# A convolution phase's written plan: statistics wanted a tile ahead, new durations, and two rows moved into the last product of an MLP

## The chip, the cores and the metric

The kernel runs on one core of one Trainium2 chip. The metric is the device time of one execution in microseconds: 9876.48 us is the median of three runs of the kernel before (9865.71 to 9877.53). The profiled execution spans 9870.0 us.

## What is computed

The input is x of 64 x 96 images of 56 x 56 pixels, in float32. Layer 0 is normalized in groups of three channels, and each of the 6144 images gets its own 7 x 7 filter from a small MLP over its own pixels; the filtered image is added to x. The kernel keeps g alone: adding x is adding the group's deviation to the middle tap and its mean to the bias. Layer 1 (a Fourier mixer and a quantized feed-forward) follows on the result. Only layer 0 is touched here:

```python
g = gn(x)                                       # groups of 3 channels: (x - m) / sqrt(s + eps)
a = g.reshape(b, c, h * w)
a = (a - mu) * rsqrt(var + EPS) * ln_gamma + ln_beta
a = gelu(einsum('bcn,nd->bcd', a, w0) + b0)     # 3136 pixels -> 512
weight = (einsum('bcd,dk->bck', a, w1) + b1).reshape(b * c, 1, 7, 7)
out = conv_general_dilated(g, weight, padding=3, feature_group_count=b * c)
return x + out + attn_bias
```

## The kernel before, in words

`conv_layer` (L299) works on tiles of 126 images, 49 of them (the last has 96), one image per partition. A tile goes through these steps; the names are the functions inside `tile_` (L364):

- **load** brings 126 x 3136 pixels into `x` (two buffers) and a bias column into `sm`, a tile of twelve columns of per-image numbers (four buffers).
- **The statistics** are a chain of small steps over four engines. `stats` x7 and `aggregate` (VectorE) give mean and variance per image; `group_mean` (TensorE, L405) averages over three channels; `spread` (VectorE); `group_variance` (TensorE, L415); `deviation` (ScalarE, a square root, L420); `scales` (VectorE, L425 to L429); `deviation2` (ScalarE, a second root, L432); `inverse2`; `norm` (ScalarE, L438) rewrites the whole of `x`; `rows` (TensorE, L443) turns three columns of `sm` into rows, and `keep_rows` (VectorE) puts them into the tile `rows`. The GELU comes later on ScalarE from another table set, so each tile loads the table for the root and the one for the GELU anew.
- **turn(k)** and **keep_turned(k)**, k from 0 to 6: TensorE transposes four slices of 112 pixels of `x`, ScalarE copies them into `xT` (one buffer).
- **hidden(k)**: the MLP's first product, four of 28 matmuls over 112 pixels each, summed in the bank `pm` (L474). With k = 0 comes one matmul ahead of them (L470): the three rows of `rows` against `rows0`, which brings in mean, bias and scale. `gelu`, `turn_hidden`, `keep_hidden`, `taps`, `keep_taps` make the 49 taps of each image.
- **The convolution by Fourier transforms**: `over_y(k)` (L519) transforms along one axis; `keep_y` and `store_y` write to a scratch tensor in HBM (`turn_x`). For four blocks q: `load_y`, `filter_spectrum` (L537, spectrum of the taps), `over_x` (L565), four products on VectorE (`times`, L572), two sums on GpSimd (`join`, L580), `back_x` (L590), `store_x` to a second scratch tensor (`turn_y`). For seven chunks c: `load_x` into `V` (two buffers), `back_y` (L613), `finish`, `store`.

Banks of PSUM: six under the tag `ps` that turn, over_y, filter, over_x, back_x and back_y share, one for `pm`, one for the small results of the statistics (`pg`).

The order is made in two steps. `Plan` (L167) is a planner in the kernel: `add` takes a step with a due time `when`, an engine, a cost, what it reads and writes, and a `lag` until its result can be used. `emit` keeps a clock of its own and always calls, on each free engine, the ready step with the earliest due time, if its buffers fit and its due time is no more than `ahead` past the earliest step not yet begun. Only the order of the calls comes out of it; nothing waits for a planned time. The recording layer below then makes the semaphores, and places instructions on each engine's queue by its own order of readiness, so that an instruction can stand elsewhere in its queue than its call stood. On the chip each queue is worked through as it stands.

In the plan before, tile i is due from T = 62 i, the statistics are due from T - 25 to T - 10 with costs from 0.15 to 0.85 us (the root with its table load 0.3), and all seven turns from T - 8 to T - 2.

## Time and profile before

| what | value | from |
|---|---|---|
| median of three runs | 9876.48 us | times |
| TensorE busy, whole span | 93% | page, part 1 |
| VectorE, ScalarE, GpSimd busy | 46%, 45%, 17% | page, part 1 |
| 0 to 4300 us: TensorE busy, granted clock | 3849.67 us, 0.85 | table by stage |
| 4300 to 9870 us: TensorE busy, granted clock | 5341.72 us, 0.96 | table by stage |
| matmuls of `hidden` (L474) | 2744 records of 595 ns | page, part 5 |
| mean share of the DMA engines, 0 to 4300 us | 0.42 | table by stage |

A group of instructions reads: line, engine, operation, what it writes and reads, shape, count, then busy time and mean of one, then the idle time of its engine just before it and what ended that. In the list of waits each line is who waited, for whom, the total, the count and the longest. A float32 matmul shows as two records. PE is TensorE, PEld its weight loads, DVE VectorE, ACT ScalarE, POOL GpSimd; SPq is the queue from which the transfers are issued. The granted clock is the share of full speed that TensorE was given. The line numbers of the changed kernel are 4 to 17 higher than before.

### The profile page before, as it was taken

The page shows a single profiled execution, that of the slowest core. Times are in us where ns is not written, and L with a number is a line of the kernel's source. Part 1 is how long each engine was busy: PE and PEld are TensorE (multiplying, and loading weights), DVE is VectorE, ACT ScalarE, POOL GpSimd, SP SyncE. Part 2 cuts the span into 40 slices and gives each one's busy share as a digit, 9 for nine tenths or more (in the row PEclk, how much of TensorE's full clock was granted, in tenths as well). Part 3 has the DMA queues.
Part 4 walks back from the last instruction along what each step waited for, and adds up shares of the span by engine and source line. Part 5 has one row for each costly group of instructions (what it writes and reads, how often), then busy time and mean ns, then how long its engine had stood idle before and what let it go on. Part 6 is the DMA issues. An engine that isn't in the chain of part 4 may idle for free.

```text
span 9870.0 us, 164798 instructions
## 1 busy us (share of the span) xinstructions
PE 9191.4 (93%) x62665; PEld 5769.7 (58%) x62665; DVE 4517.7 (46%) x11547; ACT 4424.6 (45%) x9809; POOL 1691.7 (17%) x1804
## 2 busy tenths in 40 slices
PE   7899999988999889989999999999999999999998
PEld 3545555554554455556666666666666666666665
DVE  2222222222222222225666666666666666666666
ACT  2222222222222222225555555555555555555555
POOL 0111111111111111111222222222222222222222
PEclk9888888888888888869999999999999999999999
DMA  3444444444444444443444444444444444444443
GB/s 105 126 125 122 116 121 121 122 120 126 125 115 119 119 121 122 122 116 107 121 122 120 123 118 124 121 115 119 122 121 123 121 121 121 123 118 118 121 120 94
DMA packets 1164289, 1178.26 MB, mean 119 GB/s; under 512 B 673247, under 2 KB 1075455, under 8 KB 1150932
## 3 DMA queue, kind: packets, MB, share of 16 engines
q1 hardware_dynamic: 1152643, 1160.72, 42.8%
q10 hardware_dynamic: 10858, 7.01, 0.3%
q8 instruction: 498, 8.16, 0.3%
q14 instruction: 290, 2.38, 0.1%
HBM read 589.36 MB, written 578.03 MB: 118 GB/s over the span
## 4 chain that ended last, share of the span: by engine, by line
PE 84%; ACT 5%; DMA 5%; DVE 3%; POOL 1%; issue 1%; ACTq 0%; DVEq 0%; SPq 0%; POOLq 0%
PE pm L474 11%; PE s L1037 8%; PE h L906 6%; PE pf L537 6%; PE s L954 5%; PE s L565 4%; PE s L590 4%; DMA V<-turn_y 4%; PE s L1108 4%; PE c L1197 4%; PE quarters L873 4%; PE s L1113 3%; PE y L1184 3%; PE m L1300 3%; PE m L1322 3%; PE s L1126 3%
## 5 line engine op out<-in xcount | busy, mean ns | idle before, releaser
L474 PE MATMUL pm<-w0g,xT 112*126 112x512 f32 (+1 forms) x2744 | 1242.2, 595 | 46.2 <-ACT xT L463 46.2
L572 DVE TENSOR_TENSOR t<-s,W 128x504 f32<-128x504 f32 (+1 forms) x784 | 490.9, 673 | 1610.1 <-PE s L565 1129.6
L580 POOL TENSOR_TENSOR t<-t,t 128x504 f32<-128x504 f32 (+1 forms) x392 | 485.2, 1245 | 3796.4 <-DVE t L572 3793.3
L474 PEld LDWEIGHTS pm<-w0g,xT 112*126 112x126 f32 (+1 forms) x2744 | 511.2, 188 | 693.4 <-issue 637.4
L1037 PE MATMUL s<-dft,Y 112*128 112x112 f32 (+1 forms) x7552 | 884.1, 299 | 6.1 <-ACT t L963 3.4
L1037 PEld LDWEIGHTS s<-dft,Y 112*128 112x128 f32 (+1 forms) x7552 | 741.2, 182 | 160.3 <-issue 117.9
L1341 POOL TENSOR_TENSOR o<-t,y 96x448 f32<-96x448 f32 x448 | 502.9, 1129 | 1404.7 <-DVE y L1332 1384.1
L906 PE MATMUL h<-w1c,t 96*56 96x193 f32 x3584 | 729.1, 340 | 0.0
L905 PE MATMUL h<-w1c,t 96*64 96x193 f32 x3584 | 722.3, 341 | 0.0
L620 ACT ACTIVATE o<-s,sm 126x448 f32<-126x448 f32 (+1 forms) x343 | 217.6, 634 | 1098.5 <-PE s L613 883.7
L526 DVE COPY A<-s 128x504 f32<-128x504 f32 (+1 forms) x343 | 232.8, 679 | 1041.4 <-PE s L519 1041.4
L1307 ACT CAST h<-m 128x448 f16<-128x448 f32 x1344 | 672.5, 539 | 76.4 <-PE m L1300 62.7
L938 DVE SCALAR_TENSOR_TENSOR g<-h,st,nb 120x192 f32<-120x192 f32 x1792 | 623.4, 410 | 11.5
L893 POOL TENSOR_TENSOR sq<-t 96x448 f32<-96x448 f32 x448 | 466.9, 1047 | 943.4 <-PE quarters L873 685.1
L1310 DVE TENSOR_SCALAR h<-h,fb 128x448 f16<-128x448 f16 x1344 | 458.7, 342 | 369.2 <-ACT h L1307 329.0
L537 PEld LDWEIGHTS pf<-wT,spec 49*128 49x128 f32 x3136 | 543.5, 268 | 128.7 <-issue 111.8
L954 PE MATMUL s<-g,dft 56*64 56x192 f32 x7168 | 583.1, 349 | 21.3 <-DVE t L1191 19.6
L1058 POOL TENSOR_SCALAR w<-w 128x448 f32<-128x448 f32 (+3 forms) x512 | 248.1, 485 | 2026.8 <-DVE w L1052 1743.6
L1052 DVE SCALAR_TENSOR_TENSOR p<-s,pa,p 128x448 f32<-128x448 f32 (+3 forms) x512 | 273.4, 534 | 689.6 <-ACT r L1049 525.9
L537 PE MATMUL pf<-wT,spec 49*128 49x126 f32 (+1 forms) x3136 | 581.0, 362 | 0.4 <-ACT wT L512 0.4
L545 ACT COPY W<-pf 128x504 f32<-128x504 f32 (+1 forms) x392 | 226.2, 577 | 759.8 <-PE pf L537 759.8
L1108 PE MATMUL s<-w2b,CD 128*112 128x192 f32 x1920 | 519.0, 352 | 5.0 <-DVE CD L1052 3.1
(166 smaller groups left out, 17088.0 us busy)
## 6 DMA issues: line engine op xcount, KB each, us to landing
turned<-t SPq DMA_DIRECT2D x896, 180.0 KB
Y<-turned SPq DMA_DIRECT2D x768, 168.0 KB
turn_x<-A SPq DMA_DIRECT2D x336, 252.0 KB
Y<-turn_x SPq DMA_DIRECT2D x768, 110.2 KB
turn_y<-B SPq DMA_DIRECT2D x192, 441.0 KB
V<-turn_y SPq DMA_DIRECT2D x336, 252.0 KB
U<-turned SPq DMA_DIRECT2D x448, 180.0 KB
t<-x SPq DMA_DIRECT2D x448, 168.0 KB
```

Source lines behind the costliest of these rows:

```text
L474: nc.tensor.matmul(v["pm"][:n], v["xT"][:, e * ROWS : e * ROWS + n], w0g[:, e], start=False, stop=e == HALF - 1,)
L537: nc.tensor.matmul(v["pf", q, r][:, f * ROWS : f * ROWS + n], spec[:, q, f, r], v["wT"][:, :n], start=True, stop=True,)
L572: nc.vector.tensor_tensor(blocks(v["t", q, r, s]), blocks(v["s2", q, r][:, : 4 * ROWS]), blocks(v["W", q][:, s]), ALU.mult,)
L580: nc.gpsimd.tensor_tensor(blocks(v["t", q, *a]), blocks(v["t", q, *a]), blocks(v["t", q, *b]), ALU.add if r else ALU.subtract,)
L905: nc.tensor.matmul(out_[:64], rows_[:, :64], moving, start=True, stop=True)
L906: nc.tensor.matmul(out_[64 : 64 + S], rows_[:, S : 2 * S], moving, start=True, stop=True)
L938: nc.vector.scalar_tensor_tensor(v["g"][:, j], v["ps"][:TOK, j, :H1], v["st"][:, 1, j : j + 1], nb1[:TOK], ALU.mult, ALU.max,)
L954: nc.tensor.matmul(v["pd", wp][64 * half : 64 * half + 64, i], dft1[rows_, 4 * c + j], v["g"][rows_, j], start=True, stop=True,)
L1037: nc.tensor.matmul(to_, v["Y"][:, k, channels], dft2, start=True, stop=k0 + k > 0,)
L1108: nc.tensor.matmul(two, cdb, w2b, start=True, stop=False)
L1307: nc.scalar.copy(v["h16", c][:, m], v["u", c, m])
L1341: nc.gpsimd.tensor_tensor(o, t, y, ALU.add)
```

## The change

Three things are done, all in `conv_layer`.

1. **Statistics a tile ahead.** The load is due at T - 85 in place of T - 60, the statistics from T - 72 to T - 40 with gaps between the steps, so that each small step has time to come back before the next engine needs it. `ahead` grows from 110 to 260.
2. **New durations and times.** Costs and lags are set anew (the root with its table load 1.6, TensorE steps with a lag of 0.2). A tile is due every 70 us instead of 62. The turns, the transforms along y and the products of the MLP are spread evenly, one group of each every 8.6 us, and the later steps follow from there. Only the first turn now opens `xT`, so turning no longer waits in the plan for the products before it.
3. **Mean and bias rows in the last product.** L470 goes. The last of the 28 products takes 114 rows instead of 112: `place_rows`, a transfer of two rows of up to 126 numbers on the SP queue, puts two rows of `rows` under the last slice of `xT`, and once, at the start, two rows of `rows0` are put under the last slice of `w0g`. The third row of `rows0` is zero and is left out.

The diff, cut to its core:

```diff
-    plan = Plan(BUFS1, ahead=110.0)
+    plan = Plan(BUFS1, ahead=260.0)
...
-        w0g = cp.tile([RI, HALF, HID0], F32, name="w0g")
+        w0g = cp.tile([RI + 2, HALF, HID0], F32, name="w0g")
...
+        nc.sync.dma_start(w0g[RI:, HALF - 1], rows0[:2])
...
+            def place_rows():
+                nc.sync.dma_start(
+                    v["xT"][RI:, (HALF - 1) * ROWS : (HALF - 1) * ROWS + n], v["rows"][:2, :n]
+                )
...
             def hidden(k):
                 if k == 0:
                     v["pm"] = bank(f"pm{i}", "mlp")
-                    nc.tensor.matmul(
-                        v["pm"][:n], v["rows"][:, :n], rows0, start=True, stop=False
-                    )
                 for e in range(4 * k, 4 * k + 4):
+                    p = RI + 2 if e == HALF - 1 else RI
                     nc.tensor.matmul(
-                        v["pm"][:n], v["xT"][:, e * ROWS : e * ROWS + n], w0g[:, e],
-                        start=False, stop=e == HALF - 1,
+                        v["pm"][:n], v["xT"][:p, e * ROWS : e * ROWS + n], w0g[:p, e],
+                        start=e == 0, stop=e == HALF - 1,
                     )
...
+            def pe(when, cost, step, **kw):
+                add(when, "PE", cost, step, lag=0.2, **kw)
...
-            add(T - 60, "SP", 0.6, load, w=[xs, sm], lag=12.0)
+            add(T - 85, "SP", 0.7, load, w=[xs, sm], lag=8.5)
             for j in range(NCHUNK):
-                add(T - 25 + j, "DVE", 0.62, lambda j=j: stats(j), r=[xs], w=[st])
+                add(T - 72 + j, "DVE", 0.56, lambda j=j: stats(j), r=[xs], w=[st])
...
-            add(T - 17, "PE", 0.2, group_mean, r=[sm], w=[pg])
-            add(T - 16, "DVE", 0.5, spread, r=[pg], w=[sm])
-            add(T - 15, "PE", 0.2, group_variance, r=[sm], w=[pg])
-            add(T - 14, "ACT", 0.3, deviation, r=[pg], w=[sm])
-            add(T - 13, "DVE", 0.85, scales, w=[sm])
-            add(T - 12, "ACT", 0.3, deviation2, w=[sm])
-            add(T - 11.5, "DVE", 0.18, inverse2, w=[sm])
-            add(T - 11.8, "ACT", 2.95, norm, r=[sm], w=[xs])
-            add(T - 11, "PE", 0.15, rows, r=[sm], w=[pg])
+            add(T - 62, "PE", 0.35, group_mean, r=[sm], w=[pg], lag=1.5)
+            add(T - 58, "DVE", 0.7, spread, r=[pg], w=[sm], lag=0.5)
+            add(T - 55, "PE", 0.35, group_variance, r=[sm], w=[pg], lag=1.5)
+            add(T - 51, "ACT", 1.6, deviation, r=[pg], w=[sm], lag=0.3)
+            add(T - 48, "DVE", 0.8, scales, w=[sm], lag=0.3)
+            add(T - 46, "ACT", 0.3, deviation2, w=[sm], lag=0.3)
+            add(T - 44, "DVE", 0.18, inverse2, w=[sm])
+            add(T - 40, "ACT", 3.05, norm, r=[sm], w=[xs], lag=0.3)
+            add(T - 43, "PE", 0.2, rows, r=[sm], w=[pg], lag=1.0)
...
-                add(T - 8 + k, "PE", 0.7, lambda k=k: turn(k), r=[xs], w=[pt, nm("xT")])
-                add(T - 7 + k, "ACT", 0.6, lambda k=k: keep_turned(k), r=[pt],
-                    w=[nm("xT")] + [("xTpart", i, k)])
+                pe(T - 9 + K * k, 0.6, lambda k=k: turn(k), r=[xs],
+                   w=[pt, nm("xT")] if k == 0 else [pt])
+                if k == 0:
+                    add(T - 6, "SP", 0.4, place_rows, r=[nm("rows"), nm("xT")],
+                        w=[("xTrows", i)], lag=2.5)
+                add(T - 8 + K * k, "ACT", 0.58, lambda k=k: keep_turned(k),
+                    r=[pt, nm("xT")], w=[("xTpart", i, k)])
...
-                add(T + 3 * k, "PE", 3.5 + (0.9 if k == 0 else 0),
-                    lambda k=k: hidden(k), r=[nm("xT"), xTk, nm("rows")], w=[nm("mlp")])
+                pe(T + K * k, 3.6, lambda k=k: hidden(k),
+                   r=[nm("xT"), xTk] + ([("xTrows", i)] if k == NCHUNK - 1 else []), w=[nm("mlp")])
...
-                Q = T + 34 + 14 * q
+                Q = M + 12 + 15 * q
...
-                R = T + 108 + 8.5 * c
+                R = M + 12 + 60 + 16 + 8.6 * c
...
-            tile_(i, 62.0 * i)
+            tile_(i, 70.0 * i)
```

Here K is 8.6 and M is T + 6.5 K + 4, the time at which the GELU is due.

## The prediction

> **What bounds the kernel now.** I read the page first (busy shares, clock row), then the table by stage, then the waits of one long stretch, then the timeline of one tile. The page says TensorE:

> ```profile
> span 9870.0 us, 164798 instructions
> PE 9191.4 (93%) x62665; PEld 5769.7 (58%) x62665; DVE 4517.7 (46%) x11547; ACT 4424.6 (45%) x9809; POOL 1691.7 (17%) x1804
> PEclk9888888888888888869999999999999999999999
> ```

> VectorE and ScalarE are below half busy. The convolution takes the first 17 to 18 slices, about 4300 us, and there the granted clock is 8 tenths against 9 later. The change lies in that phase. The second phase's order of TensorE instructions is the same in both built programs, so I leave its 5550 us alone.

> The waits from 500 to 4000 us, which hold 40 tiles (columns: total us, times, longest):

> ```profile
> PE pg L443 <- ACT sm L432: 150.5, 38, 4.0
> ...
> PE s L613 <- DMA V<-turn_y: 72.5, 40, 3.6
> ...
> PE pm L474 <- ACT xT L463: 40.9, 41, 1.0
> ...
> PE pg L415 <- DVE sm L412: 28.0, 40, 0.7
> ```

> Per tile TensorE stands still 3.96 us at L443 (158.4 us of idle time in the group of L443, two waits filed under the DMA included, over 40), 1.81 for the first loads of V, 1.02 for xT, 0.70 at L415, 0.3 elsewhere: 7.8 us. L443 starts 12 times between 1506.3 and 2459.6 us, so a tile takes 86.7 us. How the 3.96 arises, in the timeline:

> ```profile
> 1586.88 1.28 ACT L420 ACT_TABLE_LOAD   x1
> ...
> 1587.67 0.59 PE L415 MATMUL pg<-sm,group 126*126 126x1 f32 x2 [0.70 <-DVE sm L412]
> 1588.29 0.26 ACT L420 ACTIVATE sm<-pg,eps 126x1 f32<-126x1 f32 x1
> ...
> 1588.98 3.00 ACT L438 ACTIVATE x<-x,sm 126x3136 f32<-126x3136 f32 x1 [0.42 <-DVE sm L426]
> ...
> 1592.22 0.37 PE L443 MATMUL pg<-ident,sm 126*3 126x126 f32 x1 [3.96 <-ACT sm L432]
> ...
> 1592.52 3.63 PE L565 MATMUL s<-Y,fwd_x 112*64 112x504 f32 x8
> ```

> L405, L415 and L443 stand back to back on TensorE, and ScalarE runs the 3.00 us normalization ahead of the small root (L432, 0.28 us, ends at 1592.16) that L443 needs. The table load is already over when L415 ends. The last line shows a second cost: eight records of L565 take 3.63 us here, 1.91 at 1525.23. Windows of 4 us (seventh column: clock):

> ```profile
> 1588.00:1592.00 4.00, 0.26 (x2) 0.17 (x1) 0.52 (x4) 3.44 (x4) 0.00 (x0) 0.50 0.79 173
> ...
> 1604.00:1608.00 4.00, 4.00 (x13) 2.03 (x11) 0.00 (x0) 0.58 (x1) 0.00 (x0) 0.50 0.00 0
> ...
> 1612.00:1616.00 4.00, 4.00 (x11) 1.60 (x11) 1.42 (x3) 0.00 (x0) 2.45 (x2) 1.00 0.68 177
> ```

> The clock is whole or half, and stays at half well after the stall.

> [...]half-clock stretches last 7 to 9 times 3.41 us per tile, with a single full window inside some. It starts before the L443 wait, after the last hidden product, in a run of back_y, L470, the V wait and transposes; and filter_spectrum alone (L537) doesn't end it, over_x and back_x do.[...]

> Price of half clock: mean clock in the phase is 0.845, so 2 x 0.155 = 31% of 86.7 = 26.9 us per tile at half. Some 5 of these are waiting; 21.9 are work, which takes 1.85 times as long (3.71/1.95 back_x, 3.78/2.05 filter, 3.63/1.91 over_x), so 21.9 x (1 - 1/1.85) = 10.1 us per tile are lost.

> **The change, part by part.** What counts is the changed program's order on each engine, for nearly every tile (here tile 12 of the steady part; L409, L419, L447 are the old L405, L415, L443):

> ```
> PE   L544 filter q0 (tile 11) | L481 hidden(1) x4 (12) | L409 L419 L447 (13) | L620 back_y 0 (10)
>      | L460 turn 2, L526 over_y 2 (12) | L597 back_x q0 (11) | L620 | L460 | L544 filter q1 | L481 hidden(2)
> ACT  L424 LoadActFuncSet [waits PE] | L424 root | L442 normalize | L436 root | L627 | L467 xT
> ```

> *Due times and durations of the statistics.* They should pull the five small steps apart; the built order does not follow. The three matmuls are still adjacent, and the normalization is still ahead of the second root. Worse, the table load now carries the wait on L419, so its 1.28 us no longer hide: 3.96 + 1.28 = 5.24 us, and 0.70 before. Everything on TensorE queues behind it. Bounds: 3.96 (load hidden after all) to 5.3; I take 5.24.

> *V.* In before the late V loads queue behind the 1543 KB x load (V issued at 1574.60, used at 1581.92). In the new order the V load for block 6 is issued ahead of x, and the first ones about 10 us of TensorE work before use (filter 2.05, hidden 3.6, statistics). The wait goes: -1.81.

> *xT.* over_y 2 directly follows turn 2 and waits for its copy: 1.0 us, as before. Other copies have 1.2 to 6 us of work between. back_x has 5 us or more of TensorE work against about 4.4 for four products (0.68) and a join (1.25): 0.1.

> Idle: 0.70 + 5.24 + 1.02 + 0.1 = 7.1 against 7.8: gain 0.7 us per tile.

> *The removed matmul L470*: 1.12 us in the timeline (1579.71), every tile, on the bounding engine: gain 1.1. Two more rows in the last of 28 products cost nothing: a product's 595 ns come from its 512 columns. The new transfer of two rows has no price of its own in the trace; between a queue slot of 0.3 us and the 7.3 us that the x load needs (1573.73 to 1581.01), it is wanted only by hidden(6), some 60 us of TensorE work after hidden(0), so nothing. The wait of its issue on hidden(6) of the tile before holds the SP queue (behind it: a store of B, loads of Y and V), which have over 10 us.

> *The clock.* The low stretch now starts when hidden(1) ends: 0.58 + 0.70 + 0.58 + 5.24 + 0.37 = 7.5 us[...]. But dense work follows sooner. At half rate: back_y 1.9, turn 1.1, wait 1.0, then over_y 2.2 and back_x 3.7, dense from 11.5 to 17.4. A window of which three quarters were dense released the clock in before, so release falls at 14.2 to 17.7, mean 16. That is 11.4 us at half, 3.5 of them idle; 7.9 x 0.46 = 3.6 us lost. Two new stretches (back_y, turn, filter: 1.03 + 0.6 + 2.05 = 3.7 us)[...]; a quarter each at 2.5 us: 1.3. Lost 4.9 against 10.1: gain 5.2, the largest and least sure term.

> Sum: 0.7 + 1.1 + 5.2 = 7.0 us per tile. The first three tiles have another order; 46 x 7.0 = 322 us. 9876.5 - 322 = 9554, say 9555. Ends of the phase: the last tile's chain is the same steps with a few more back_y in between; nothing.

> **Rivals.**
> 1. [...]2 x 2.5 instead of 1.3, clock gain 1.5. 3.3 x 46 = 152: 9725. For: filter alone closed it. Against: 2.7 us of filter and turn never did.
> 2. [...]gain 0.7 + 1.1 + 10.1 = 11.9, 547 us: 9330. Against: 7.5 us without dense work.
> 3. The statistics wait vanishes as the due times intend: idle 1.1, so 6.7 + 1.1 + 10.1 = 17.9, 823 us: 9053. The order speaks against it.
> 4. Slower: two of the next tile's statistics now stand ahead of the four products of q3 on VectorE and wait for the x load. It needs 7.3 us; the order gives about 10 from turn 6 to the products. If it comes 4 us late, back_x of q3 waits[...]: 7.6 against 7.0, so +28: 9904.

> **How the numbers follow.** Main 0.62, rival 1 0.17, rival 2 0.08, rival 3 0.03, rival 4 0.10 (a part of it within 0.2%, 20 us). Predicted 9555. Range 9400 to 9750: takes in rival 1 and half the way to rival 2, leaves out 0.2. Faster 0.88 (main, 1, 2, 3, less a little), same 0.04, slower 0.08.

> **What would show it.** Right: a wait of about 5.2 us at L447 on the second root, with the table load inside it; no V wait; the xT wait at 1.0; mean clock of the phase near 0.91; tiles of about 79.7 us. Wrong: tiles under 76 us with no wait at L447 (rival 3), clock still near 0.85 (rival 1), or a long wait of back_x on POOL (rival 4).

## The result, and the profile after

The changed kernel takes 9464.63 us (median; 9452.38 to 9472.47) against 9871.09 us for the kernel before, measured beside it: a ratio of 0.9588, 95% interval 0.9571 to 0.9605. The forecast was 9555 us with a range of 9400 to 9750: right in direction and inside the range, 90 us too slow.

The page of the changed kernel first: its span, TensorE's busy time, and the granted clock in 40 slices.

```profile
span 9457.8 us, 164686 instructions
...
PE 8851.2 (94%) x62567; PEld 5498.1 (58%) x62567; DVE 4521.8 (48%) x11547; ACT 4409.0 (47%) x9809; POOL 1687.8 (18%) x1804
...
PEclk9999999999999999799999999999999999999999
```

The convolution phase now ends at 3899 us instead of 4307. TensorE is as full as before, with 340 us less of busy time, although it issues only 49 matmuls less (98 records, two for each): most of what went is the same work, done faster. The clock row says why, since its first part held mostly 8s before.

TensorE's waits between 500 and 3500 us (who waits, for whom, total us, times, longest):

```profile
PE pg L447 <- ACT sm L436: 206.7, 39, 5.3
PE pg L419 <- DVE sm L416: 27.3, 39, 0.7
PE s L526 <- ACT xT L467: 26.1, 39, 0.7
PE s L597 <- POOL t L587: 0.7, 2, 0.4
```

No wait for V is left. The wait on the second root did not go: it grew to 5.3 us in every tile. The timeline of one tile shows it whole (start, duration, engine, line; in brackets the idle time before it and what ended that). L481 is hidden, L419 and L447 are the second and the third small matmul, L424 and L436 the two roots, L442 is the normalization, L526 over_y, L597 back_x:

```profile
1516.60 3.70 PE L481 MATMUL pm<-w0g,xT 112*126 112x512 f32 x8
...
1521.11 0.38 PE L419 MATMUL pg<-sm,group 126*126 126x1 f32 x2 [0.70 <-DVE sm L416]
...
1521.57 1.28 ACT L424 ACT_TABLE_LOAD   x1 [4.29 <-PE pg L419]
...
1523.55 3.00 ACT L442 ACTIVATE x<-x,sm 126x3136 f32<-126x3136 f32 x1 [0.42 <-DVE sm L430]
...
1526.46 0.28 ACT L436 ACTIVATE sm<-sm,eps 126x1 f32<-126x1 f32 x1
...
1526.79 0.37 PE L447 MATMUL pg<-ident,sm 126*3 126x126 f32 x1 [5.30 <-ACT sm L436]
...
1530.35 2.05 PE L526 MATMUL s<-xT,fwd_y 112*128 112x504 f32 x2 [0.67 <-ACT xT L467]
...
1532.33 3.71 PE L597 MATMUL s<-t,inv_x 64*112 64x504 f32 x8
...
1551.10 1.95 PE L597 MATMUL s<-t,inv_x 64*112 64x504 f32 x8
```

The table load starts only when L419 is done, and the normalization (3.00 us) runs ahead of the second root. The same back_x takes 3.71 us just behind the stall and 1.95 us twenty us later. The table by stage around it (stretch, length, then busy us of PE, PEld, DVE, ACT, POOL with counts, then the clock, the DMA share and GB/s):

```profile
1516.00:1520.00 4.00, 4.00 (x14) 2.09 (x14) 2.54 (x4) 0.97 (x2) 1.85 (x2) 1.00 1.00 236
...
1524.00:1528.00 4.00, 1.21 (x7) 1.21 (x7) 0.44 (x2) 2.74 (x2) 0.00 (x0) 0.50 0.00 0
...
1532.00:1536.00 4.00, 4.00 (x10) 1.13 (x9) 0.68 (x1) 0.00 (x0) 0.00 (x0) 0.50 0.18 67
1536.00:1540.00 4.00, 4.00 (x31) 3.76 (x30) 0.00 (x0) 2.78 (x6) 0.00 (x0) 0.89 0.32 75
```

In both traces the clock is whole or half, and within each all changes lie on a grid of 3.41 us (230 records before, 192 after); a window in what follows is one step of that grid. The clock is whole ahead of the stall, falls within it, and is back three or four windows after the fall, 10.2 or 13.7 us; over_y, over_x, back_x and hidden take at least 0.71 of the last low window (39 low stretches). In the kernel before, the filter that followed stood in the low stretch too, with 9.0 us of its work at half clock per tile.

**Where the 412 us between the two spans went.** I cut both traces at the starts of the third small matmul (L443, L447), and took from each stretch TensorE's busy time, the time that the records show at half clock, and the part of it that was busy. At 1.85 times the duration (the prediction's price), busy time at half clock loses 0.46 of itself. In the whole convolution phase, busy time at half clock fell from 1060 to 413 us: 647 x 0.46 = 298 us. Idle time fell from 453 to 382 us: 71. The second phase gave 4, and 39 are left for the removed matmul and what this split can't place. So some three quarters of the gain is the clock.

### The profile page after: what moved, and what is told of

It is laid out like the page before. It is cut to its first block, busy times and chain, and to the rows that moved or that the text cites. A ratio compares the mean times of both kernels' runs of the same rounds, so it can differ in the third digit from the quotient of the medians.

```text
span 9457.8 us, 164686 instructions
## 1 busy us (share of the span) xinstructions
PE 8851.2 (94%) x62567; PEld 5498.1 (58%) x62567; DVE 4521.8 (48%) x11547; ACT 4409.0 (47%) x9809; POOL 1687.8 (18%) x1804
## 4 chain that ended last, share of the span: by engine, by line
PE 88%; ACT 4%; DVE 3%; issue 3%; DMA 2%; POOL 0%; SPq 0%; ACTq 0%; POOLq 0%; DVEq 0%
PE pm L481 12%; PE s L1054 8%; PE h L923 6%; PE s L971 5%; PE s L597 5%; PE s L526 4%; PE pf L544 4%; PE s L1125 4%; PE c L1214 4%; PE s L620 4%; PE quarters L890 4%; PE s L1130 4%; PE s L572 4%; PE y L1201 3%; PE m L1317 3%; PE m L1339 3%
## 5 line engine op out<-in xcount | busy, mean ns | idle before, releaser
L481 PE MATMUL pm<-w0g,xT 112*126 112x512 f32 (+2 forms) x2744 | 1245.3, 596 | 0.0
L481 PEld LDWEIGHTS pm<-w0g,xT 112*126 112x126 f32 (+2 forms) x2744 | 491.4, 187 | 534.4 <-issue 523.0
L627 ACT ACTIVATE o<-s,sm 126x448 f32<-126x448 f32 (+1 forms) x343 | 217.3, 633 | 922.6 <-PE s L620 583.2
L955 DVE SCALAR_TENSOR_TENSOR g<-h,st,nb 120x192 f32<-120x192 f32 x1792 | 623.3, 409 | 11.5
L606 ACT COPY B<-s 112x504 f32<-112x504 f32 (+1 forms) x392 | 208.1, 579 | 770.0 <-PE s L597 762.8
L1066 ACT ACTIVATE p<-s,pa 128x448 f32<-128x448 f32 (+3 forms) x512 | 267.3, 522 | 539.2 <-PE s L1054 538.8
L1130 PE MATMUL s<-w2a,CD 128*112 128x96 f32 x3712 | 510.7, 259 | 0.0
```

The source lines that it names most:

```text
L481: nc.tensor.matmul(v["pm"][:n], v["xT"][:p, e * ROWS : e * ROWS + n], w0g[:p, e], start=e == 0, stop=e == HALF - 1,)
L955: nc.vector.scalar_tensor_tensor(v["g"][:, j], v["ps"][:TOK, j, :H1], v["st"][:, 1, j : j + 1], nb1[:TOK], ALU.mult, ALU.max,)
L1130: nc.tensor.matmul(two[:, e * C : (e + 1) * C], cda, w2a, start=False, stop=k == ks[-1],)
```

## The experiments

**The theories.** *Clock theory*, the prediction's own with more weight: the gain is mostly work that no longer runs at half clock, because dense products (hidden, over_y, over_x, back_x, with about 500 columns each) follow the one stall of a tile sooner; the new due times of the statistics don't remove the stall. *Statistics theory*: that the statistics are wanted a tile ahead is the gain. *Rows theory*: the removed matmul and what queued behind it is the gain.

All tiles in one table. The time is the median of a kernel's runs; the rest is the mean of 40 tiles of its profiled run, from the sixth start of the third small matmul to the 46th, in us per tile; "work" is the busy time less 0.46 of the busy time at half clock.

| kernel | time, us | tile | idle | at half clock | of it busy | work |
|---|---|---|---|---|---|---|
| before | 9871.1 | 86.39 | 7.94 | 27.34 | 22.42 | 68.14 |
| after | 9464.6 | 78.13 | 6.78 | 12.42 | 8.47 | 67.46 |
| e1_keep_row_matmul | 9497.3 | 78.49 | 6.12 | 10.23 | 8.42 | 68.50 |
| e2_rows_only | 9759.5 | 83.37 | 8.30 | 21.50 | 16.77 | 67.35 |
| e3_shift25 | 9347.8 | 75.69 | 6.30 | 7.42 | 4.63 | 67.26 |
| e4_stat_times_only | 9736.1 | 83.31 | 7.52 | 20.85 | 17.11 | 67.93 |
| e5_small_matmuls_pinned | 9018.9 | 68.07 | 0.97 | 0.00 | 0.00 | 67.09 |
| e6_norm_pinned | 9336.9 | 75.09 | 4.93 | 8.28 | 5.99 | 67.41 |
| e7_stall_filled | 9669.0 | 81.91 | 6.75 | 10.23 | 7.26 | 71.82 |
| e7b_stall_filled_late | 9350.2 | 75.60 | 3.26 | 3.93 | 3.86 | 70.57 |
| e9_before_pinned | 9710.7 | 83.31 | 4.41 | 24.43 | 23.71 | 67.99 |
| e10_chunks_half_apart | 9268.2 | 73.45 | 4.72 | 6.91 | 5.21 | 66.33 |
| e11_pinned_turns_earlier | 9005.9 | 67.98 | 0.69 | 1.02 | 1.00 | 66.84 |

Read the last column first. Among kernels with the row matmul (before, e1, e4, e9) it is 67.9 to 68.5, among those without it and without filler 66.3 to 67.5, while their tiles run from 68 to 83 us. What differs between the kernels is idle time and half clock, hardly the work.

### The parts of the change alone

*The row matmul put back*; the two rows under the last slice and their transfers are gone again.

```diff
...
                 if k == 0:
                     v["pm"] = bank(f"pm{i}", "mlp")
+                    nc.tensor.matmul(
+                        v["pm"][:n], v["rows"][:, :n], rows0, start=True, stop=False
+                    )
...
```

> The changed kernel with its third part undone: the matmul of mean and bias rows (L470 of before) opens the MLP's sum again, with three rows, and the transfer that placed the rows is gone. Clock theory (most of the gain is work that no longer runs at half clock, because dense products follow the statistics' stall sooner): only the matmul comes back, 1.1 us in each of 46 tiles, so 9465 + 50 = 9515 us, between 9480 and 9550. Rows theory (the matmul and what stood behind it in TensorE's queue was the gain): at least half of the 406 us come back, 9670 us or more. Statistics theory: as the clock theory, 9515.

Measured: 9497.32 us, ratio to before 0.9611 (0.9597 to 0.9626), inside the band that the clock and the statistics theory share; 33 us came back, not half of the gain. Work per tile rose by 68.50 - 67.46 = 1.04 us, the matmul's 1.1. Its waits show why not all of that reaches the time:

```profile
PE pg L446 <- ACT sm L435: 201.4, 38, 5.3
PE s L528 <- ACT xT L466: 25.4, 38, 0.7
```

The 0.7 us wait of the second small matmul is absent: in this order hidden products stand between the first two. The rows theory falls.

*The rows alone, on the old plan* (the third part of the change's diff, applied to the kernel before).

> The kernel before with the third part alone: the two rows ride in the last product, the plan is the old one. Clock theory: 1.1 us for each of 46 tiles, 9871 - 50 = 9821 us, between 9790 and 9850, with TensorE's clock in the first phase at 0.85 as before. Rows theory: 9670 us or less. Statistics theory: as the clock theory.

Measured: 9759.49 us, ratio 0.9884 (0.9861 to 0.9908): 114 us less by the ratio, against 50 expected and over 200 for the rows theory. Neither had it. The order of the tiles changed with the edit and isn't the same from tile to tile (a wait on the first small matmul, L406, of up to 7.8 us in 14 tiles, no V wait in many). Idle time per tile is even 0.36 us longer than in the kernel before; the gain is 5.65 us less busy time at half clock, 2.6 us, and 0.8 us of work, the matmul's part. The size of an edit's own work does not bound its effect when it also reorders a queue.

*The times of the statistics alone, on the old plan*: the load at T - 85, statistics from T - 72 to T - 40 with the new durations, `ahead` 260; all products as in the kernel before.

```diff
-    plan = Plan(BUFS1, ahead=110.0)
+    plan = Plan(BUFS1, ahead=260.0)
...
-            add(T - 17, "PE", 0.2, group_mean, r=[sm], w=[pg])
+            add(T - 62, "PE", 0.35, group_mean, r=[sm], w=[pg], lag=1.5)
...
-            add(T - 15, "PE", 0.2, group_variance, r=[sm], w=[pg])
+            add(T - 55, "PE", 0.35, group_variance, r=[sm], w=[pg], lag=1.5)
...
```

> The kernel before with only the new times and durations of the load and the statistics and the longer look ahead (260); the products keep their old times, and the matmul of rows stays. Statistics theory (the statistics wanted a tile ahead are the gain): all but the matmul's 50 us, so 9515 us, at most 9600. Clock theory: the order of the products around the stall decides; the small matmuls still stand within one stall (two of the three side by side), the wait for L443 stays at 3 to 5 us a tile, and at most the 1.8 us wait for V and the 0.7 us for the second small matmul go, with some clock: 9700 to 9880 us.

Measured: 9736.06 us, ratio 0.984 (0.9812 to 0.9868). The statistics theory (9600 or less) falls; the clock theory's band holds. Its waits:

```profile
PE pg L443 <- ACT sm L432: 199.6, 36, 5.5
PE pg L405 <- DVE sm L399: 70.8, 36, 3.7
```

V's wait went, but the stall on the second root is 5.5 us, and the first small matmul now waits 2 us for VectorE: idle time fell by 0.4 us only; most of the gain is clock, (22.42 - 17.11) x 0.46 = 2.4 us a tile. This run also measures the price of half clock without any model. Its tiles come in short ones and long ones. Of the 40, the 24 with under 20 us at half clock have a mean of 80.4 us with 10.8 us busy at half clock, the other 16 a mean of 87.7 us with 26.5 us. (87.7 - 80.4) / (26.5 - 10.8) = 0.46; a line through all 40 has the slope 0.47. That is close to the prediction's 0.46, from another kernel in another way.

*The statistics wanted 25 us later, in the changed kernel*:

```diff
-            add(T - 62, "PE", 0.35, group_mean, r=[sm], w=[pg], lag=1.5)
+            add(T - 37, "PE", 0.35, group_mean, r=[sm], w=[pg], lag=1.5)
...
-            add(T - 55, "PE", 0.35, group_variance, r=[sm], w=[pg], lag=1.5)
+            add(T - 30, "PE", 0.35, group_variance, r=[sm], w=[pg], lag=1.5)
...
```

> The changed kernel with the statistics (not the load) wanted 25 us later in the plan: T - 47 to T - 15 in place of T - 72 to T - 40. In TensorE's queue the three small matmuls still stand side by side, now behind two dense hidden groups instead of one. Clock theory: what counts is the work around the one stall, not how early the statistics are wanted; the stall stays at 5.3 us with dense products ahead of and behind it, 9465 us give or take 60. Statistics theory (being wanted a tile ahead is the gain): a part of the 406 us comes back, 9550 us or more, and a wait for V or for x shows up again on TensorE.

Measured: 9347.82 us, ratio 0.9478 (0.9457 to 0.9499): 117 us faster than the changed kernel, outside both bands, and on the far side of the statistics theory's. The stall stayed (the wait on the second root is 5.3 us in the mean, 5.6 at the longest); what I had not worked out is the order behind it. There, over_y (L526) and back_x (L597) follow at once after a single back_y (L620), with no turn and no wait for its copy, and back_x runs at full clock:

```profile
1564.83 0.37 PE L447 MATMUL pg<-ident,sm 126*3 126x126 f32 x1 [5.30 <-ACT sm L436]
1564.99 1.95 PE L620 MATMUL s<-inv_y,V 128*126 128x112 f32 x8
1566.74 1.64 PE L526 MATMUL s<-xT,fwd_y 112*128 112x504 f32 x2
1568.31 1.95 PE L597 MATMUL s<-t,inv_x 64*112 64x504 f32 x8
```

Half clock fell from 12.42 to 7.42 us a tile: (8.47 - 4.63) x 0.46 = 1.8, and 0.5 of idle time, 2.3 of the 2.44 us that a tile gained. So not how early the statistics are wanted, but what stands next to the stall. This is the clock theory's mechanism, with a size that I should have worked out from the order. The new times of the products alone were not run; what they bring is read from the order.

### Is it the stall that lowers the clock?

*Filler in the stall, first try.* Seven dense matmuls, whose result nothing reads, behind the second small matmul:

```diff
+FILL = 7
...
                 nc.tensor.matmul(
                     v["pg"][:n, 1:2], group[:n, :n], col(3), start=True, stop=True
                 )
+                for _ in range(FILL):
+                    nc.tensor.matmul(
+                        v["pg"][:, 136:512], fwd_y, w0g[:RI, 0, :376], start=True, stop=True
+                    )
```

> The changed kernel with work added that nothing needs: seven dense matmuls (112 rows by 376 columns) behind the second small matmul of each tile, which fill the 5.3 us that TensorE waits there; what the kernel computes is unchanged. Clock theory: the wait isn't shortened, but TensorE is no longer seen idle, so the half-clock stretch of 12.4 us a tile goes, or shrinks to one window of 3.4 us: 8.5 us of busy time at half clock give 3.9 us a tile back, 46 x 3.9 = 180 us, so 9285 us, at most 9380, and the clock of the first phase rises from 0.92 to 0.98 or more. If the clock has another cause than the idle stretch (the small-weight products around it, say): 9465 us or up to 240 us more, where the added work (about 5 us at full clock, 10 at half) outlasts the wait.

Measured: 9668.97 us, ratio 0.9779 (0.9763 to 0.9795), slower than the changed kernel by 204 us. It did not do what it was built for. The timeline (in this kernel L420 is the second small matmul, L424 the filler, L429 the root, L452 the third small matmul):

```profile
1518.64 0.38 PE L420 MATMUL pg<-sm,group 126*126 126x1 f32 x2 [0.70 <-DVE sm L417]
...
1518.88 4.67 PE L424 MATMUL pg<-w0g,fwd_y 112*128 112x376 f32 x14
...
1523.62 1.28 ACT L429 ACT_TABLE_LOAD   x1 [8.81 <-PE pg L424]
...
1528.84 0.37 PE L452 MATMUL pg<-ident,sm 126*3 126x126 f32 x1 [5.29 <-ACT sm L441]
```

The root reads the bank that the filler writes, so it waits for all seven; the stall of 5.3 us stands behind the filler instead of under it. That leaves one thing learned: 4.67 us of dense work just ahead of the stall don't keep the clock up. Half clock is still 10.23 us a tile, against 12.42 without them. The time lies in the band of the clock theory's rival (9465 us and up to 240 us more), but the filler stands outside the stall, so this run doesn't decide between the two.

*Second try.* The filler is issued behind the root, five of them; now it waits for the root, and the root for nothing new.

```diff
+FILL = 5
...
                     col(7), v["pg"][:n, 1:2], AF.Sqrt, bias=eps[:n], scale=1.0
                 )
+                for _ in range(FILL):
+                    nc.tensor.matmul(
+                        v["pg"][:, 136:512], fwd_y, w0g[:RI, 0, :376], start=True, stop=True
+                    )
```

> The changed kernel with work added that nothing needs, five dense matmuls (112 rows by 376 columns, 0.67 us each in the run e7_stall_filled); what the kernel computes is unchanged. They write the bank that the square root L424 reads, so they start when that is done, some 2.2 us into the 5.3 us wait, and end about when L447 may start: the wait's idle time falls from 5.3 us in one piece to about 2.2, and nothing needed is held up. Clock theory: the half-clock stretch of 12.4 us a tile goes or shrinks to one window of 3.4: 2.5 to 3.9 us a tile, 115 to 180 us, so 9285 to 9350 us, and the clock of the first phase is 0.96 or more. If the clock has another cause: 9450 to 9500 us with the same stretch of low clock.

Measured: 9350.17 us, ratio 0.9478 (0.9455 to 0.9501): 114 us faster than the changed kernel, with 5 needless matmuls more in each tile, at the slow end of the clock theory's band and far from the 9450 to 9500 of its rival. In the timeline L425 is the root, L429 the filler:

```profile
1558.78 0.38 PE L420 MATMUL pg<-sm,group 126*126 126x1 f32 x2 [0.70 <-DVE sm L417]
...
1559.24 1.28 ACT L425 ACT_TABLE_LOAD   x1 [4.29 <-PE pg L420]
...
1560.85 5.12 PE L429 MATMUL pg<-w0g,fwd_y 112*128 112x376 f32 x10 [1.69 <-ACT sm L425]
...
1565.80 0.27 PE L452 MATMUL pg<-ident,sm 126*3 126x126 f32 x1
```

The idle piece is 1.69 us instead of 5.30. The clock still falls, but for one window of 3.4 us (two in 6 of the 40 tiles), which here lies over the filler (five at 1.02 us, against 0.67 in the first try), and L452 runs at full speed again. Busy time at half clock went from 8.47 to 3.86 us. What the tile needs was not done earlier: L452 comes 7.02 us after the start of L420, against 5.68 us in the changed kernel. Only the clock behind it is better. So the idle stretch is what brings the half clock here: with dense work in it, 3.93 us a tile are at half clock in place of 12.42.

*The small matmuls held apart.* All three, in the changed kernel:

```diff
-                nc.tensor.matmul(
+                tc.keep_in_program_order(nc.tensor.matmul(
                     v["pg"][:n, :1], group[:n, :n], col(0), start=True, stop=True
-                )
+                ))
...
```

(and the same around `group_variance` and `rows`). Each now stands on TensorE's queue behind what the plan called before it.

> The changed kernel with the three small matmuls held in TensorE's queue at the places that the plan gives them, with several products between the first, the second and the third, in place of side by side. Clock theory: the waits for L416 (0.7 us) and L436 (5.3 us) go, and with the idle stretch the half-clock stretch (8.5 us of busy time, 3.9 us lost) goes too: up to 9.9 us for each of 46 tiles, 455 us, so 9010 us; 9100 us if half of the low stretch stays. If the small-weight products and not the stall hold the clock low: only the 6.0 us of idle time go, 9190 us, and the clock of the first phase stays at 0.92. If another wait takes the stall's place: about 9465 us.

Measured: 9018.88 us, ratio to before 0.9146 (0.9122 to 0.917), 446 us faster than the changed kernel; the clock theory had 9010. From the table by stage (500 to 3300 us) and the waits:

```profile
500.00:3300.00 2800.00, 2760.04 (x12388) 1475.70 (x12387) 829.50 (x1684) 985.40 (x1564) 405.21 (x328) 1.00 0.52 153
```

```profile
PE s L528 <- ACT xT L469: 34.0, 42, 0.8
```

A clock of 1.00: there is no half clock in any of the 40 tiles, although the same filters and back_y products run. No wait on a statistics step is left. 78.13 - 68.07 = 10.06 us a tile, of which idle time is 5.81 and the clock 8.47 x 0.46 = 3.90.

### How far the order must go

*The normalization behind the second root* (ScalarE's queue alone; the three small matmuls stay side by side):

```diff
-                nc.scalar.activation(
+                tc.keep_in_program_order(nc.scalar.activation(
                     v["x"][:n], v["x"][:n], AF.Identity, bias=col(9), scale=col(8)
-                )
+                ))
```

> The changed kernel with the normalisation of x (L442, 3.0 us) held in ScalarE's queue behind the second square root L436, in place of ahead of it; TensorE's queue keeps the three small matmuls side by side. If the 5.3 us wait is made up as the prediction had it (table load 1.28, square root, VectorE, normalisation 3.0, second square root), it falls to 2.3 us. Clock theory: the half-clock stretch then shrinks too, from 12.4 us to at most two windows of 3.4: 3.0 us of idle time and 1.5 to 3.9 us of clock, 46 x (4.5 to 6.9) = 205 to 315 us, so 9150 to 9260 us. If the clock doesn't depend on the idle stretch: 138 us, 9327 us. If ScalarE's order isn't what sets the wait: 9465 us.

Measured: 9336.85 us, ratio 0.9467 (0.9453 to 0.9481): 128 us faster than the changed kernel, where at least 205 was expected. The waits:

```profile
PE pg L447 <- ACT sm L436: 101.5, 40, 2.5
PE s L526 <- ACT xT L467: 60.6, 39, 2.3
```

The stall fell from 5.30 to 2.54 us, so its make-up was read rightly. But the 3.0 us normalization now stands ahead of the copy that over_y waits for, and that wait rose from 0.7 to 1.55 us in the mean. Idle time fell by 1.85 us instead of 3.0, and half clock to 8.28 us, two or three windows of 3.4, instead of two at most. The time alone would also fit the rival in which the clock doesn't depend on the idle stretch (9327 us); the trace tells the two apart, since of the 3.04 us that a tile gained 1.85 are idle time and (8.47 - 5.99) x 0.46 = 1.14 are clock.

*The chunks of turn, over_y and hidden 4.3 us apart in the plan instead of 8.6*:

```diff
-            K = 8.6
+            K = 4.3
...
-            M = T + K * 6.5 + 4
+            M = T + 8.6 * 6.5 + 4
```

> The changed kernel with the chunks of turn, over_y and hidden planned 4.3 us apart in place of 8.6 (the rest of a tile's plan where it was). In TensorE's queue this alone parts the three small matmuls: four hidden matmuls stand between the first and the second, and some 25 products between the second and the third. Clock theory: no stall of 5.3 us, so no half-clock stretch from it: near e5_small_matmuls_pinned, 9010 to 9150 us. Statistics theory: the statistics' due times are unchanged, so 9465 us. If the spacing of the chunks (dense hidden products between sparse ones) is itself what keeps the clock up: the low stretch returns where filters and back_y products come together, at most 6.0 us a tile of idle time gained and some lost again, 9250 to 9465 us.

Measured: 9268.17 us, ratio 0.9392 (0.9371 to 0.9412), faster than the changed kernel by 196 us. The statistics theory (9465) falls once more; of the other two bands it lies in that of the third, but not for the reason given there:

```profile
1522.01 0.28 PE L419 MATMUL pg<-sm,group 126*126 126x1 f32 x2
...
1522.37 1.28 ACT L424 ACT_TABLE_LOAD   x1 [12.99 <-PE pg L419]
...
1524.36 3.00 ACT L442 ACTIVATE x<-x,sm 126x3136 f32<-126x3136 f32 x1 [0.43 <-DVE sm L430]
...
1527.78 0.57 ACT L467 COPY xT<-pt 112x504 f32<-112x504 f32 x1
...
1528.40 2.05 PE L526 MATMUL s<-xT,fwd_y 112*128 112x504 f32 x2 [4.70 <-ACT xT L467]
```

No small matmul waits. The table load, the root and the normalization now hold up a copy of xT in ScalarE's queue, over_y waits for it for 4.70 us, and the clock falls there (2.05 us for the L526 that takes 1.01 at full clock). The same ScalarE work came back as a stall through another queue. The work column is 1 us lower than its kin; I have no reason for that.

*The pins alone, on the old plan* (the diff of e5 applied to the kernel before).

> The kernel before with the three small matmuls held apart in TensorE's queue where its old plan has them (behind a hidden group; behind hidden; behind the taps' products), nothing else. Clock theory: the stall in one piece goes or is cut, but the old plan still puts three filter groups one behind the other with few dense products near, and the kernel before ran those at half clock: 4 to 5 us of idle time and up to 3 us of clock a tile, 9500 to 9690 us, and the clock of the first phase stays below 0.92. If the stall alone had held the clock low: 0.98 and 4.7 + 10.1 us a tile, about 9200 us. If another wait takes its place: 9800 us or more.

Measured: 9710.65 us, ratio 0.9845 (0.9829 to 0.9862), 20 us slower than the slow end of the clock theory's band (9690). Idle time fell from 7.94 to 4.41 us a tile; the clock didn't gain at all, 23.71 us of busy time at half clock against 22.42. The timeline shows what holds it down (L615 is back_y, L539 the filter, L592 back_x):

```profile
1515.35 1.10 PE L615 MATMUL s<-inv_y,V 128*126 128x112 f32 x8 [1.94 <-DMA V<-turn_y]
...
1525.84 7.19 PE L539 MATMUL pf<-wT,spec 49*128 49x126 f32 x32
...
1533.99 3.78 PE L539 MATMUL pf<-wT,spec 49*128 49x126 f32 x16
1537.57 3.40 PE L592 MATMUL s<-t,inv_x 64*112 64x504 f32 x8
```

A wait for V, then back_y, the taps' small products and three filters in a row. The clock falls at 1516.6, behind 3.4 us of which 1.94 were the wait for V; in each of the 40 tiles the first low stretch follows a window of 3.4 us with 1.5 us or more of idle time. Then it stays low with TensorE nearly always busy, and here it rises only in back_x; in 10 tiles it rises for one window in between and falls again with no idle time before it. So the wait for V, which grew from 1.8 to 2.6 us (94.8 over 36), has taken over the start of the low stretch, and the sparse products its length. Taken off the new plan, the pins bring 150 us; on it, 446. The pins, which part the small matmuls, bring the larger sum only on the plan that also ends the wait for V and spreads dense products between the filters; which of these two matters more was not parted.

*The pins, and the turns 2 us earlier in the plan*:

```diff
-                pe(T - 9 + K * k, 0.6, lambda k=k: turn(k), r=[xs],
+                pe(T - 11 + K * k, 0.6, lambda k=k: turn(k), r=[xs],
...
-                add(T - 8 + K * k, "ACT", 0.58, lambda k=k: keep_turned(k),
+                add(T - 10 + K * k, "ACT", 0.58, lambda k=k: keep_turned(k),
```

> The kernel of e5_small_matmuls_pinned with one more edit: the turns and the copies of xT are wanted 2 us earlier, so that a statistics step, a hidden group or a back_y stands between every turn and the over_y that needs its copy. In e5 that wait (L528 on ScalarE's copy) was 0.8 us a tile. If it goes and nothing takes its place: 46 x 0.8 = 37 us off 9019, 8982 us. If another wait takes it, or the low clock comes back with the new order: 9019 us or more.

Measured: 9005.86 us, ratio 0.9147 (0.9127 to 0.9166); beside e5's 0.9146 no difference can be told. The wait of over_y for its copy went, a wait of hidden for a copy took most of its place (0.6 us), and 1.0 us a tile at half clock came back (one window in each of 12 tiles, behind a filter, a turn and that wait). e5 and e11 are the fastest kernels here, both 8.5% below the kernel before and, by the two ratios, 4.6% below the changed one.

## Why the prediction was right, and where its size was off

*Which edit brings what.* Right in the main: the prediction expected the largest part from the clock, read from the built order and not from the intent of the due times, and e4 and e3_shift25 bear that out.

*Due times of the statistics.* Right. The stall was put at 5.24 us with the table load inside; it is 5.30, and e6 confirms its make-up. TensorE ran its queue as built: in all 40 tiles the lines start in the order L481, L409, L419, L447, L620, L460, L526, L597, L620, L460, L544, L481, and the L620 behind L447 starts 0.16 to 0.17 us after it, with no wait of its own.

*V.* Right: no wait of TensorE for V in 500 to 3500 us. e4 shows the same without the new product times, so it belongs to the new times of the load and the statistics or to the longer look ahead, which that run has too.

*xT and POOL.* 1.02 and 0.1 us predicted, 0.67 and nearly nothing measured. With 7.94 us of idle time a tile before (7.8 taken) and 6.78 after (7.1 predicted), the idle term gave 1.16 instead of 0.7 us.

*L470.* 1.1 predicted; e1 shows 1.04 us of work. Between before and after the work column differs by 0.68, so 0.4 us of it can't be placed by this split. The two rows more cost nothing, as said: a record with 114 rows takes 592 ns, one with 112 rows 596, and the old L470, with 3 rows and the same 512 columns, took 646 in the kernel before. The columns do count: in e7, 14 records of 376 columns take 4.67 us, 0.33 each, and 8 of 512 columns take 3.70 us in the changed kernel, 0.46 each.

*The clock.* This was called the least sure term, and it is the mis-sized one. Its main stretch was good: 11.4 us at half clock with 7.9 busy predicted, 12.42 with 8.47 measured, 3.9 us lost instead of 3.6. Where that stretch begins was my estimate, not shown by a trace: with the rise put at 16 us behind hidden(1), 16 - 11.4 = 4.6 us behind it. In the changed kernel the fall comes 3.3 us behind hidden(1) in the mean (2.0 to 5.3 in 40 tiles), the rise 15.6. That three quarters of dense work in a window bring the rise is shown in part: in the kernel before, the last window of a low stretch was dense to 0.76 or more, but five windows with 0.77 to 0.83 were followed by another low one. The second part of the term failed: 1.3 us for two new stretches (back_y, turn, filter: 3.7 us each), also an estimate. In none of the 40 tiles did the clock fall there: each has one stretch of three or four windows, around L447. Set to 0, and with 22.42 x 0.46 = 10.3 us lost before instead of 10.1, the clock term is 6.4 instead of 5.2.

*The sum and the tiles.* 7.0 us per tile predicted, 8.26 measured: 1.16 idle, 6.42 clock, 0.68 work. The work term, 0.4 too large, hid a part of the other two, 0.5 and 1.2 too small. The clock of the phase is 0.92 and a tile 78.13 us, against 0.91 and 79.7. Times 46 that is 380 of the 412 us. The other 32 were put at nothing, in "Ends of the phase": the drain behind the last L447 is 27.7 us shorter. Its busy time at half clock fell from 52.4 to 27.0 us and its idle time from 22.6 to 18.0, together 25.4 x 0.46 + 4.6 = 16 us; the other 11 are mostly work that the new order does ahead of that L447 (781 records of TensorE stand behind it, 811 before), so a cut there shows the ends only roughly. The last tiles' chain has the same steps, as the prediction said, but its clock rises too, which it left out. Of the 90 us that the forecast missed, 46 x 1.26 = 58 are the tile and some 30 the ends and the start from 9876 instead of 9871 us.

*The rivals.* 1, the clock low in both new stretches of every tile, falls (no further low stretch). What spoke for it did happen in the kernel before, where 12 of 51 falls follow a window with 3.1 to 3.4 us of filter work. 2, hardly any half clock left, falls (the clock drops in every tile). 3 falls for the change as it is, but its arithmetic stands: it had 9053 us for tiles without the statistics wait and without half clock, and e5, which makes that so, takes 9019. 4 falls: VectorE does wait for the x load,

```profile
DVE stats L394 <- DMA x<-in_x_dram: 126.6, 38, 5.2
```

by 3.3 us in the mean, but TensorE's waits show back_x waiting 0.7 us in 39 tiles together.

## What to carry to other kernels

When small dependent steps stand side by side on one engine's queue, wanting them earlier in a plan moves the stall but does not part them: look at the built order, and hold them apart with independent work between each pair (446 us here, more than the whole change). Price a stall on TensorE with the half clock behind it, not by its length alone: here 6.0 us of stall cost some 10 (5.81 of idle time and 3.90 of clock in e5), and dense products closer behind it cut the bill (e3). And when a step is moved on one engine, ask what stands behind it there; e6 and e10 gave back part of their gain because a copy that TensorE needs stood behind the moved ScalarE work.
